# Linear attention with a soft mixture of experts: GpSimd's whole-group operations in halves, x's bias a group ahead, largest logits by way of memory, other ranks

## The chip, the cores and the metric

The kernel runs on one core of a Trainium2 chip. The metric is the device time of one execution in microseconds (us), as the median of several runs. A core has five engines that matter here, each with its own in-order instruction queue: TensorE (PE), VectorE (DVE), ScalarE (ACT), GpSimd (POOL) and SyncE (SP); SP only issues DMA transfers in this kernel. Weight loads of PE are listed apart as PEld.

## The reference

The input x holds 4 sequences of 2048 tokens with 256 channels, all in float32. What is computed, cut to what matters:

```python
def mlp(x, W1, b1, W2, b2): return gelu(x @ W1 + b1) @ W2 + b2          # erf gelu
q, k, v = mlp(x, ..q), mlp(x, ..k), mlp(x, ..v)
scores = einsum('bid,bjd->bij', q, k) / sqrt(256 * 512) * tril(ones)    # no softmax
out = einsum('bij,bjd->bid', scores, v)
out = layernorm(out) * ln_w + ln_b
x = layernorm(x + out)                        # no weights
xn = layernorm(x) * gamma + beta
logits = einsum('bnd,des->bnes', xn/|xn| * scale, mu/|mu|)   # 16 experts x 16 slots
dispatch = softmax(logits, over the tokens n)
combine  = softmax(logits, over all 256 slots)
slot_in  = einsum('bnd,bnes->besd', xn, dispatch)
slot_out = gelu(slot_in @ w1[e] + b1[e]) @ w2[e] + b2[e]     # hidden width 64
out = einsum('besd,bnes->bnd', slot_out, combine)
x = layernorm(x + out)                        # the result, 4 x 2048 x 256
```

The softmax over the tokens needs, for each of the 256 slots, the largest logit of a whole sequence.

## The kernel before

The tokens are worked on in 16 groups of 512 (four groups to a sequence), each group as four tiles of 128 tokens by 256 channels. Attention without a softmax is linear: a running sum of k and v products (`state`) stands for all earlier groups, so that only the 128×128 blocks on the diagonal need scores of their own.

For each group t the kernel calls

- `attend(t)`: the three two-layer networks (first layers L802 on PE, gelu L812 on ACT; second layers L825 for k and L852 for v, taken out of PSUM by DVE at L835 and L863), the scores (L877), the state (L904, L920), the sums of the columns (L937), which go to memory and come back to all partitions (L946, L952, L957, L961) and are added up by GpSimd (L971), and the output (L987, L991), which DVE takes out of PSUM (L1002), measures (L553, L554) and centres and scales with ln_w (L1014);
- `norms(t)`: GpSimd adds ln_b to x in `row` (L1030) and sets a column of ones (L1033); DVE adds the attention to it (L1047); two layer norms follow, of which GpSimd makes the product with gamma (L1106) and the sum with beta (L1114) that give `xn`; ACT takes the sums of the squares (L1125);
- `back(t)`: the logits (L1171) and what the softmaxes need of them (L1193, L1204, L1221), kept negative in `lg`, their smallest values so far in `mx`, and the numerators `ct` of the combine softmax, which are turned round through memory.

After the fourth group of a sequence, `softmaxes(groups)` turns `mx` on PE (L1246), reduces it on DVE to one value for each of the 256 slots (`cm`, two columns of 128 partitions, L1254), and brings these to all partitions: `spread` multiplies the identity by each column (L677, DVE, twice) and multiplies it on PE by a matrix of ones (L683), and ACT copies the product out of PSUM into `dg` (L1271). GpSimd then subtracts `dg` from each group's `lg` (L1282), and ACT takes exp (L1294). `slots` sums over the tokens on PE (L1316), runs the experts (L1368, L1392, L1411, L1438, L1447), and `finish(t)` combines (L1542 on PE, L1550 on DVE), normalises and stores (L1500).

The order of the work isn't written out. Every operation is a step of a planner, `plan.step(engine, length, emit, reads, writes)`, with a rank: `plan.begin(base)` sets the base, and each step takes the base plus 0.01 for each step before it. `Plan.run()` goes through the steps before the program runs, picks for every engine the ready step with the lowest sum of start time and rank times PATIENCE (0 for the engines that compute, where the rank decides between equal starts; 1.0 for SP), with the lengths that the steps carry and an assumed delay LATE from one engine to the next, and so writes down five in-order queues. A step that reads PSUM gets its rank lowered by 1.5. Buffers (`row` has 8 places, `xT` 2, `dg` 1) are given out in the same pass.

The main loop sets the bases; the lines around the change are

```python
attend(t)                                                  # base t
plan.begin(t + (TAIL["norms"] if last else 0.6)); norms(t)
plan.begin(t + 0.3);                              load_x(t + 2)
plan.begin(t + (TAIL["back"] if last else 1.1));  back(t)
```

At the end of a sequence follow `softmaxes` (base t + 1.4), `slots` (t + 1.7) and `finish` of its four groups (from t + 2.6 in steps of 0.2). The last two sequences have bases of their own in TAIL. In the last sequence `softmaxes` is called twice: for its first three groups, and for the last group alone, whose subtraction goes tile by tile to the engines in SUBTRACT. CENTERS says for each of the last eight groups which engine normalises which tile in `finish`. `load_x(t)` issues one load of `row` and eight loads of `xT` on SP.

Of the kernel before, what the change touches and what calls it, by code (L numbers as in the profile page):

```python
# [10 lines left out]
ALU = mybir.AluOpType  # L11
# [6 lines left out]

PIECES = ((2, False), (2, True))

CENTERS = [['ACT', 'ACT', 'ACT', 'ACT'], ['ACT', 'DVE', 'DVE', 'DVE'], ['ACT', 'ACT', 'ACT', 'ACT'], ['DVE', 'DVE', 'DVE', 'DVE'], ['ACT', 'DVE', 'ACT', 'DVE'], ['ACT', 'DVE', 'DVE', 'DVE'], ['ACT', 'ACT', 'ACT', 'ACT'], ['DVE', 'DVE', 'ACT', 'DVE']]

SUBTRACT = ['DVE', 'POOL', 'DVE', 'POOL']

TAIL = {'norms': 0, 'back': 0.3, 'softE': 1.4, 'part': 2.2, 'soft': 1.0, 'slots2': 4.6, 'fin2': [5.5, 0.3], 'slots3': 1.7, 'fin3': [2.6, 0.2], 'table': 1.0}
LAST = 2
W = G * P
LN_EPS = 1e-5
NORM_EPS = 1e-12
# [25 lines left out]

class Plan:

    LATE = {"PE": 0.45, "DVE": 0.25, "ACT": 0.25, "POOL": 0.25, "SP": 3.5, "IN": 0.0}
    TABLE = 1.3

    PATIENCE = {"PE": 0.0, "DVE": 0.0, "ACT": 0.0, "POOL": 0.0, "SP": 1.0, "IN": 0.0}

    def __init__(self):
        self.steps, self.places, self.order, self.free = [], {}, {}, set()
# [16 lines left out]
        self.order[tag].append(b)  # L81
        return b

    def step(self, engine, length, emit, reads=(), writes=(), table=None, holds=()):


        s = Step(engine, length, emit, self.base + self.count, table)
        s.holds = list(holds)
        for b in holds:
            b.left += 1  # L90
        self.count += 0.01

        if any((a[0] if isinstance(a, tuple) else a).tag.startswith("ps_") for a in reads):
            s.rank -= 1.5
        for accesses, write in ((reads, False), (writes, True)):
            for a in accesses:
                b, parts = a if isinstance(a, tuple) else (a, range(a.parts))
                if b not in s.buffers:
                    s.buffers.append(b)
                    b.left += 1  # L100
# [12 lines left out]
        s.before.discard(s)  # L113
        s.waiting = len(s.before)
        for o in s.before:
            o.after.append(s)
        self.steps.append(s)

    def run(self):
# [25 lines left out]
        while left:  # L145
# [43 lines left out]
                    since[b.tag].append(b.last)  # L189
            for o in s.after:  # L190
                o.waiting -= 1
                seen = end + (self.LATE[e] if o.engine != e or e == "SP" else 0.0)
                o.ready = max(o.ready, seen)
                if not o.waiting:
                    ready[o.engine].append(o)
# [8 lines left out]
def _dve(n):  # L204
    return 0.155 + 0.00105 * n


def _pool(n):
    return 0.1 + 0.0022 * n
# [10 lines left out]
def kernel(  # L220
# [43 lines left out]
    for tag, n, shape in (  # L264
# [32 lines left out]
    plan.tag(  # L297
        "bounce", [memory.tile([KC, W, P], F32, name=f"bounce_{i}") for i in range(16)], True
    )
    plan.tag("sums", [memory.tile([G, C], F32, name=f"sums_{i}") for i in range(2)], True)  # L300
    bank_places("mm", 3)
    bank_places("tp", 2)
# [720 lines left out]
    def norms(t):  # L1023
# [1 line left out]


        a, row, mv = a_tiles.pop(t)
        plan.step(
            "POOL", _pool(G * C),
            lambda: nc.gpsimd.tensor_tensor(row[:, :, :C], row[:, :, :C], lnb_r, ALU.add),  # L1030
            [rows_b], [row],
        )
# [11 lines left out]
        for c in range(G):  # L1044

            def emit(c=c):
                nc.vector.scalar_tensor_tensor(  # L1047
                    row[:, c, :C], a[:, c, :], r[:, c : c + 1], row[:, c, :C],
                    ALU.mult, ALU.add, accum_out=mv2[:, c, 0:1] if t >= ACCZ else None,
                )  # L1050

            if t >= ACCZ:
                plan.step("DVE", 0.57, emit, [(a, [c]), r], [(row, [c]), (mv2, [c])])
# [47 lines left out]
                [(row, [c])], [(xn, [c])],  # L1101
            )
        if t < ngroups - 1:
            plan.step(
              "POOL", _pool(G * C),
              lambda: nc.gpsimd.tensor_tensor(  # L1106
                  by_halves(xn), row[:, :, :C].rearrange("p g (k d) -> p k g d", k=KC), gam_h,
                  ALU.mult,
              ),
              [row], [xn],  # L1110
            )
            plan.step(
              "POOL", _pool(G * C),
              lambda: nc.gpsimd.tensor_tensor(by_halves(xn), by_halves(xn), bet_h, ALU.add),  # L1114
              [], [xn],
            )
        plan.step("POOL", 1.4, emit, [rr, ve2], [sq, sc])
        xnT = None
        if by_blocks(t):
# [117 lines left out]
    def softmaxes(groups, before=None):  # L1237
# [22 lines left out]
        if before:  # L1260
# [3 lines left out]
                nc.vector.tensor_tensor(less.place, cm.place, before.place, ALU.subtract)  # L1264

            plan.step("DVE", 0.3, emit, [before], [cm, less])
        row = spread(cm)
        cmb = plan.buffer("dg")
        plan.step(
            "ACT", _act(ES),  # L1270
            lambda: nc.scalar.copy(cmb.place.rearrange("p h e -> p (h e)"), row[:, :ES]),  # L1271
            [row], [cmb],
        )
        for t in groups:

            n = 1 if t == ngroups - 1 else G
            for c in range(0, G, n):
                cs = list(range(c, c + n))
                engine = SUBTRACT[c] if n == 1 else "POOL"

                def emit(lg=l_tiles[t], c=c, n=n, engine=engine):
                    (nc.vector if engine == "DVE" else nc.gpsimd).tensor_tensor(  # L1282
# [4 lines left out]
                        ALU.subtract,  # L1287
                    )

                length = _dve(ES) if engine == "DVE" else _pool(n * ES)  # L1290
                plan.step(engine, length, emit, [cmb], [(l_tiles[t], cs)])

                def emit(lg=l_tiles[t], c=c, n=n):
# [1 line left out]
                        lg[:, c : c + n, :], lg[:, c : c + n, :], AF.Exp, scale=-1.0  # L1295
                    )

                plan.step("ACT", 1.06 if n == G else 0.38, emit, [], [(l_tiles[t], cs)], table="exp")
        if before:
            plan.step(  # L1300
                "ACT", _act(EH),
# [268 lines left out]
    for t in range(ngroups):  # L1570
# [5 lines left out]
        attend(t)  # L1576
        plan.begin(t + (TAIL["norms"] if last else 0.6))
        norms(t)
        plan.begin(t + 0.3)
        load_x(t + 2)  # L1580
        plan.begin(t + (TAIL["back"] if last else 1.1))
        back(t)
        if t == ngroups - 2:

# [5 lines left out]
            kept = part_sums(early)  # L1590
        if t % NG == NG - 1:
            groups = [t] if tail == 2 else list(range(t - NG + 1, t + 1))
            plan.begin(t + (TAIL["soft"] if tail == 2 else 1.4))
            _, less = softmaxes(groups, cm if tail == 2 else None)
            plan.begin(t + (1.7, TAIL["slots2"], TAIL["slots3"])[tail])
            so = slots(groups, kept if tail == 2 else None, less)


            first, by = ((2.6, 0.2), TAIL["fin2"], TAIL["fin3"])[tail]
            for i in range(NG):  # L1600
                plan.begin(t + first + by * i)
                finish(t - NG + 1 + i, so)
# [44 lines left out]
```

## Time and profile before

| | |
|---|---|
| time, median of 3 runs | 663.3 us (662.45 to 664.54) |
| the profiled execution | 663.13 us, span 661.4 us, mean granted PE clock 0.996 |
| busy: PE, DVE, ACT, POOL | 647.2, 490.9, 266.1, 298.5 us |
| L1030, L1106, L1114 (128×1024 on POOL) | 16 of 2.19 us, 15 of 2.18, 15 of 2.37 |
| L1282 (128×1024 on POOL) | 15 of 2.42 us |
| L1014 on DVE (128×256) | 64, mean 0.66 us |
| L683 on PE (ones times `dg`) | 12 records, 3.9 us |
| DMA | 84.7 MB, 128 GB/s over the span |

In a row of the groups of instructions stand the line, the engine, the operation, the tile written and the tile read, the shapes as partitions × elements, and the count; then the busy time in us and the mean of one in ns, and then the time in which the engine stood idle just before them, with what ended it. In a row of the timeline stand the start in us from the beginning of the span, the length in us, the engine, the line, the operation and the count; in brackets the idle time before it and what ended it. In a row of the waits stand who waited for whom, the us in total, how often, and the longest. "SPq" is an issue by SP of a DMA. The chain that ended last is followed back from the last instruction, at each step to what released it. The profile calls an operation on four tiles of a group 128×1024.

### The profile page before, as it was taken

How to read it: one execution, taken by the hardware profiler on the slowest of the kernel's cores; microseconds unless marked ns; L12 is line 12 of the kernel's file. 1: busy time of each engine (PE TensorE's matmuls, PEld its weight loads, DVE VectorE, ACT ScalarE, POOL GpSimd, SP SyncE). 2: the span in 40 equal slices, each digit the busy share in tenths (PEclk: the TensorE clock that was granted, in tenths of full speed). 3: DMA queues.
4: the chain of work that ended last, by engine and by line, in shares of the span. 5: the costliest groups of instructions: out<-in, count | busy, mean ns of one | idle time of the engine just before them, and what ended most of it. 6: DMA issues, size and time to landing. Idle time of an engine off the chain costs nothing.

```text
span 661.4 us, 9366 instructions
## 1 busy us (share of the span) xinstructions
PE 647.2 (98%) x2972; PEld 483.3 (73%) x2972; DVE 490.9 (74%) x1294; ACT 266.1 (40%) x597; POOL 298.5 (45%) x346
## 2 busy tenths in 40 slices
PE   9999999999999999999999999999999999999995
PEld 6657586777768877758686887776767768887874
DVE  1438586979797878778796388996978489886486
ACT  3130515333346227221516323634153544545475
POOL 4343616060739514353426605546061937646234
PEclk9999999999999999999999999999999999999998
DMA  8953655777577095836676525994677372621274
GB/s 247 261 123 109 129 96 130 126 152 158 99 158 128 15 199 174 188 87 128 127 130 136 87 68 91 238 212 104 109 152 133 65 160 70 83 65 32 33 160 160
DMA packets 322233, 84.71 MB, mean 128 GB/s; under 512 B 253068, under 2 KB 319944, under 8 KB 322184
## 3 DMA queue, kind: packets, MB, share of 16 engines
q1 hardware_dynamic: 321080, 83.06, 59.7%
q10 hardware_dynamic: 960, 0.80, 0.4%
q8 instruction: 23, 0.38, 0.2%
q0 software_dynamic: 144, 0.26, 0.1%
q14 instruction: 26, 0.21, 0.1%
HBM read 52.05 MB, written 32.04 MB: 127 GB/s over the span
## 4 chain that ended last, share of the span: by engine, by line
PE 92%; DVE 5%; issue 1%; POOL 1%; POOLq 0%; ACT 0%; DVEq 0%; ACTq 0%
PE mm L802 25%; PE at L904 8%; PE mm L1171 8%; PE mm L852 8%; PE at L1316 8%; PE at L1542 7%; PE at L987 7%; PE mm L825 7%; PE at L877 4%; PE at L991 4%; PE at L937 1%; PE at L461 1%; PE tp L486 1%; DVE xn L1096 1%; PE mm L683 1%
## 5 line engine op out<-in xcount | busy, mean ns | idle before, releaser
L812 ACT ACTIVATE hid<-mm,cols_sb 128x512 f32<-128x512 f32 x96 | 65.1, 686 | 142.1 <-PE mm L802 141.5
L542 POOL TENSOR_TENSOR root<-ve,nhalf 128x4 f32<-128x4 f32 (+1 forms) x39 | 40.7, 1044 | 125.1 <-DVE ve L1037 51.2
L987 PE MATMUL at<-state,hid 128*128 128x256 f32 x240 | 61.6, 379 | 0.0
L904 PE MATMUL at<-vt,kt 128*128 128x256 f32 x240 | 61.3, 385 | 0.0
L825 PE MATMUL mm<-both_sb,hid 128*128 128x257 f32 x256 | 59.5, 381 | 1.4 <-DVE kt L835 1.4
L802 PE MATMUL mm<-xT,W1v_sb 128*128 128x512 f32 x128 | 59.5, 593 | 0.7 <-DVE both_sb L770 0.7
L802 PE MATMUL mm<-xT,W1q_sb 128*128 128x512 f32 x128 | 59.5, 595 | 0.3 <-DVE xT L476 0.3
L1542 PE MATMUL at<-so,ct 128*128 128x256 f32 x256 | 57.9, 381 | 0.8 <-DVE row L1550 0.6
L1316 PE MATMUL at<-row,lg 128*128 128x257 f32 x256 | 58.2, 380 | 0.0
L1171 PE MATMUL mm<-mu_sb,xnT 128*128 128x256 f32 x256 | 58.1, 379 | 0.0
L852 PE MATMUL mm<-W2v_sb,hid 128*128 128x256 f32 x256 | 58.0, 379 | 0.0
L802 PE MATMUL mm<-xT,W1k_sb 128*128 128x512 f32 x128 | 57.7, 593 | 0.0
L825 PEld LDWEIGHTS mm<-both_sb,hid 128*128 128x128 f32 x256 | 48.2, 190 | 9.7 <-DVE kt L835 2.0
L1542 PEld LDWEIGHTS at<-so,ct 128*128 128x128 f32 x256 | 48.0, 190 | 9.9 <-issue 1.7
L1171 PEld LDWEIGHTS mm<-mu_sb,xnT 128*128 128x128 f32 x256 | 48.4, 190 | 8.4 <-issue 1.5
L987 PEld LDWEIGHTS at<-state,hid 128*128 128x128 f32 x240 | 45.6, 190 | 11.8 <-issue 5.7
L1030 POOL TENSOR_TENSOR row<-row,rows_sb 128x1024 f32<-128x1024 f32 x16 | 35.0, 2186 | 42.4 <-DMA row<-in_x_dram 33.9
L852 PEld LDWEIGHTS mm<-W2v_sb,hid 128*128 128x128 f32 x256 | 48.5, 190 | 6.7
L1221 POOL TENSOR_TENSOR sum<-sum,ss 128x4 f32<-128x4 f32 x16 | 4.0, 248 | 109.4 <-DVE ss L1217 92.9
L1316 PEld LDWEIGHTS at<-row,lg 128*128 128x128 f32 x256 | 48.1, 190 | 7.2 <-issue 0.4
L904 PEld LDWEIGHTS at<-vt,kt 128*128 128x128 f32 x240 | 44.4, 190 | 12.0 <-issue 5.4
L946 ACT COPY cs<-at 128x256 f32<-128x256 f32 (+1 forms) x16 | 5.9, 371 | 109.1 <-PE at L937 97.5
(150 smaller groups left out, 1250.8 us busy)
## 6 DMA issues: line engine op xcount, KB each, us to landing
bounce<-xn SPq DMA_DIRECT2D x30, 512.0 KB
row<-in_x_dram SPq DMA_DIRECT2D x16, 512.0 KB
ct<-bounce SPq DMA_DIRECT2D x64, 128.0 KB
bounce<-kt SPq DMA_DIRECT2D x30, 256.0 KB
kT<-bounce SPq DMA_DIRECT2D x60, 128.0 KB
out_dram<-row SPq DMA_DIRECT2D x15, 512.0 KB
xT<-in_x_dram SPq DMA_DIRECT2D x112, 64.0 KB
xnT<-bounce SPq DMA_DIRECT2D x56, 128.0 KB
```

Source lines behind the costliest of these rows:

```text
L542: nc.gpsimd.tensor_tensor(r[:, :n], v[:, :n], nhalf.to_broadcast([P, n]), ALU.pow)
L802: nc.tensor.matmul(ph.place, wa[f"W1{n}"][:, k, m * P : (m + 1) * P], xT[:, k, :], start=(k == 0), stop=(k == KC - 1),)
L812: nc.scalar.activation(hid[n][:, m, :], ph.place, AF.Gelu, bias=cols_sb[:, 4 * i + m : 4 * i + m + 1],)
L825: nc.tensor.matmul(pk[:, : C + 1], hid["k"][:, k, c * P : (c + 1) * P], wqk_sb[:, k, :], start=(k == 0), stop=(k == KC - 1),)
L852: nc.tensor.matmul(pv[:, j * C : (j + 1) * C], hid["v"][:, k, (c0 + j) * P : (c0 + j + 1) * P], wa["W2v"][:, k, :], start=(k == 0), stop=( ...
L877: nc.tensor.matmul(psc[:, toks[c]], kT[:, k, toks[c]], qT[:, k, toks[c]], start=(k == 0), stop=(k == KC - 1),)
L904: nc.tensor.matmul(pds[:, m * C : (m + 1) * C], kt[:, c, m * P : (m + 1) * P], vt[:, c, :], start=True, stop=True,)
L987: nc.tensor.matmul(po[:, :C], qT[:, k, toks[c]], s[:, k, :], start=(k == 0), stop=False,)
L1030: lambda: nc.gpsimd.tensor_tensor(row[:, :, :C], row[:, :, :C], lnb_r, ALU.add),
L1171: nc.tensor.matmul(pl[:, j * ES : (j + 1) * ES], xnT[:, k, (c0 + j) * P : (c0 + j + 1) * P], mu_sb[:, k, :], start=(k == 0), stop=(k == KC ...
L1316: nc.tensor.matmul(psi[:, : C + 1], lg[:, c, h * P : (h + 1) * P], row[:, c, :], start=(i == 0), stop=(i == n - 1),)
L1542: nc.tensor.matmul(pc[:, :C], ct[:, h, c * P : (c + 1) * P], so_t[:, h, :], start=(h == 0), stop=(h == EH - 1),)
```

## The change

Four things are changed.

- GpSimd's operations on a whole group (L1030, L1106, L1114, L1282) become two operations on two tiles each (PART = 2). Multiplication by gamma and addition of beta go half by half. The exp of L1294 is halved with the subtraction. In the last group the third of the four tiles' subtractions moves from DVE to GpSimd.
- The additions of ln_b to x get ranks that are lower by 1.0, a group ahead, and are tracked tile by tile in the planner.
- At the end of the first three sequences the 256 values of `cm` are written to memory by one DMA and read back to all 128 partitions, straight into `dg`, by another, both on SP; `spread` and ACT's copy are left out there. The planner assumes that the write takes 4.5 us longer than an ordinary step of SP. For the last sequence `spread` stays.
- Ranks: steps that read PSUM are lowered by 1.8, not 1.5; DVE's LATE is 0.3, not 0.25; SP's PATIENCE 0.5, not 1.0; `load_x(t + 2)` is at t + 0.8, not 0.3; `back` at t + 1.3, not 1.1; `softmaxes` at 1.6, not 1.4; `slots` at 2.2, not 1.7; `finish` from 2.6 in steps of 0.1, not 0.2. CENTERS has other engines for some tiles.

```diff
-CENTERS = [['ACT', 'ACT', 'ACT', 'ACT'], ['ACT', 'DVE', 'DVE', 'DVE'], ...
-SUBTRACT = ['DVE', 'POOL', 'DVE', 'POOL']
+CENTERS = [['DVE', 'ACT', 'ACT', 'ACT'], ['DVE', 'DVE', 'DVE', 'DVE'], ...
+SUBTRACT = ['DVE', 'POOL', 'POOL', 'POOL']
+PART = 2
...
-    LATE = {"PE": 0.45, "DVE": 0.25, "ACT": 0.25, "POOL": 0.25, "SP": 3.5, "IN": 0.0}
+    LATE = {"PE": 0.45, "DVE": 0.3, "ACT": 0.25, "POOL": 0.25, "SP": 3.5, "IN": 0.0}
-    PATIENCE = {"PE": 0.0, "DVE": 0.0, "ACT": 0.0, "POOL": 0.0, "SP": 1.0, "IN": 0.0}
+    PATIENCE = {"PE": 0.0, "DVE": 0.0, "ACT": 0.0, "POOL": 0.0, "SP": 0.5, "IN": 0.0}
...
-            s.rank -= 1.5
+            s.rank -= 1.8
...
-                seen = end + (self.LATE[e] if o.engine != e or e == "SP" else 0.0)
+                seen = end + s.late + (self.LATE[e] if o.engine != e or e == "SP" else 0.0)
...
+    plan.tag("mins", [memory.tile([EH, P], F32, name=f"mins_{i}") for i in range(2)], True)
...
-        plan.step(
-            "POOL", _pool(G * C),
-            lambda: nc.gpsimd.tensor_tensor(row[:, :, :C], row[:, :, :C], lnb_r, ALU.add),
-            [rows_b], [row],
-        )
+        at = plan.base, plan.count
+        plan.begin(plan.base - 1.0)
+        for c in range(0, G, PART):
+            def emit(c=c):
+                nc.gpsimd.tensor_tensor(
+                    row[:, c : c + PART, :C], row[:, c : c + PART, :C], lnb_r[:, :PART],
+                    ALU.add,
+                )
+            plan.step(
+                "POOL", 1.29, emit, [rows_b], [(row, list(range(c, c + PART)))]
+            )
+        plan.base, plan.count = at
...
+            for c in range(0, G, PART):
+                cs = slice(c, c + PART)
+                def emit_mul(cs=cs):
+                    nc.gpsimd.tensor_tensor(
+                        by_halves(xn)[:, :, cs],
+                        row[:, cs, :C].rearrange("p g (k d) -> p k g d", k=KC),
+                        gam_h[:, :, :PART], ALU.mult,
+                    )
...
+                def emit_add(cs=cs):
+                    nc.gpsimd.tensor_tensor(
+                        by_halves(xn)[:, :, cs], by_halves(xn)[:, :, cs], bet_h[:, :, :PART],
+                        ALU.add,
+                    )
...
-        row = spread(cm)
-        cmb = plan.buffer("dg")
+        if groups[-1] < ngroups - 4:
+            mins, cmb = plan.buffer("mins"), plan.buffer("dg")
+            plan.step(
+                "SP", 0.6,
+                lambda: nc.sync.dma_start(
+                    out=mins.place.rearrange("h p -> p h"), in_=cm.place
+                ),
+                [cm], [mins], late=4.5,
+            )
+            plan.step(
+                "SP", 0.5,
+                lambda: nc.sync.dma_start(
+                    out=cmb.place, in_=mins.place.partition_broadcast(P)
+                ),
+                [mins], [cmb],
+            )
+        else:
+            row = spread(cm)
+            cmb = plan.buffer("dg")
...
-            n = 1 if t == ngroups - 1 else G
+            n = 1 if t == ngroups - 1 else PART
...
-                engine = SUBTRACT[c] if n == 1 else "POOL"
+                engine = SUBTRACT[c] if t == ngroups - 1 else "POOL"
...
-                plan.step("ACT", 1.06 if n == G else 0.38, emit, [], [(l_tiles[t], cs)], table="exp")
+                plan.step("ACT", {1: 0.38, 2: 0.6, 4: 1.06}[n], emit, [], [(l_tiles[t], cs)], table="exp")
...
-        plan.begin(t + 0.3)
+        plan.begin(t + 0.8)
         load_x(t + 2)
-        plan.begin(t + (TAIL["back"] if last else 1.1))
+        plan.begin(t + (TAIL["back"] if last else 1.3))
         back(t)
...
-            plan.begin(t + (TAIL["soft"] if tail == 2 else 1.4))
+            plan.begin(t + (TAIL["soft"] if tail == 2 else 1.6))
...
-            plan.begin(t + (1.7, TAIL["slots2"], TAIL["slots3"])[tail])
+            plan.begin(t + (2.2, TAIL["slots2"], TAIL["slots3"])[tail])
...
-            first, by = ((2.6, 0.2), TAIL["fin2"], TAIL["fin3"])[tail]
+            first, by = ((2.6, 0.1), TAIL["fin2"], TAIL["fin3"])[tail]
```

More of the change, by code (lines that the diff above doesn't have):

```diff
@@ L19 @@
 PIECES = ((2, False), (2, True))
-CENTERS = [['ACT', 'ACT', 'ACT', 'ACT'], ['ACT', 'DVE', 'DVE', 'DVE'], ['ACT', 'ACT', 'ACT', 'ACT'], ['DVE', 'DVE', 'DVE', 'DVE'], ['ACT', 'DVE', 'ACT', 'DVE'], ['ACT', 'DVE', 'DVE', 'DVE'], ['ACT', 'ACT', 'ACT', 'ACT'], ['DVE', 'DVE', 'ACT', 'DVE']]
-SUBTRACT = ['DVE', 'POOL', 'DVE', 'POOL']
+CENTERS = [['DVE', 'ACT', 'ACT', 'ACT'], ['DVE', 'DVE', 'DVE', 'DVE'], ['ACT', 'DVE', 'ACT', 'DVE'], ['ACT', 'DVE', 'ACT', 'DVE'], ['ACT', 'DVE', 'ACT', 'DVE'], ['ACT', 'DVE', 'DVE', 'ACT'], ['DVE', 'ACT', 'ACT', 'ACT'], ['ACT', 'DVE', 'DVE', 'DVE']]
+SUBTRACT = ['DVE', 'POOL', 'POOL', 'POOL']
 TAIL = {'norms': 0, 'back': 0.3, 'softE': 1.4, 'part': 2.2, 'soft': 1.0, 'slots2': 4.6, 'fin2': [5.5, 0.3], 'slots3': 1.7, 'fin3': [2.6, 0.2], 'table': 1.0}
 LAST = 2
+PART = 2
 W = G * P
@@ L82, in buffer, with step @@
         return b
-    def step(self, engine, length, emit, reads=(), writes=(), table=None, holds=()):
+    def step(self, engine, length, emit, reads=(), writes=(), table=None, holds=(), late=0.0):
         s = Step(engine, length, emit, self.base + self.count, table)
-        s.holds = list(holds)
+        s.holds, s.late = list(holds), late
         for b in holds:
@@ L1052, in norms @@
             if t >= ACCZ:
-                plan.step("DVE", 0.57, emit, [(a, [c]), r], [(row, [c]), (mv2, [c])])
+                plan.step(
+                    "DVE", 0.57, emit, [(a, [c]), r], [(row, [c]), (mv2, [c])]
+                )
                 squares_of((row, [c]), mv2, c, lambda c=c: row[:, c, :C])
@@ L1103, in norms @@
         if t < ngroups - 1:
[L1104 to L1116, printed above, removed]
+            for c in range(0, G, PART):
[7 more added lines that the diff above has]
+                plan.step(
+                    "POOL", 1.29, emit_mul, [(row, list(range(c, c + PART)))],
+                    [(xn, list(range(c, c + PART)))],
+                )
[4 more added lines that the diff above has]
+                    )
+                plan.step(
+                    "POOL", 1.29, emit_add, [], [(xn, list(range(c, c + PART)))]
+                )
         plan.step("POOL", 1.4, emit, [rr, ve2], [sq, sc])
@@ L1266, in softmaxes @@
             plan.step("DVE", 0.3, emit, [before], [cm, less])
-        row = spread(cm)
-        cmb = plan.buffer("dg")
[L1269 to L1273, printed above, removed]
+        if groups[-1] < ngroups - 4:
+            mins, cmb = plan.buffer("mins"), plan.buffer("dg")
+            plan.step(
+                "SP", 0.6,
[3 more added lines that the diff above has]
+                [cm], [mins], late=4.5,
+            )
+            plan.step(
+                "SP", 0.5,
[3 more added lines that the diff above has]
+                [mins], [cmb],
+            )
+        else:
+            row = spread(cm)
+            cmb = plan.buffer("dg")
+            plan.step(
+                "ACT", _act(ES),
+                lambda: nc.scalar.copy(cmb.place.rearrange("p h e -> p (h e)"), row[:, :ES]),
+                [row], [cmb],
+            )
         for t in groups:
-            n = 1 if t == ngroups - 1 else G
+            n = 1 if t == ngroups - 1 else PART
             for c in range(0, G, n):
                 cs = list(range(c, c + n))
-                engine = SUBTRACT[c] if n == 1 else "POOL"
+                engine = SUBTRACT[c] if t == ngroups - 1 else "POOL"
                 def emit(lg=l_tiles[t], c=c, n=n, engine=engine):
@@ L1288, in emit @@
                     )
-                length = _dve(ES) if engine == "DVE" else _pool(n * ES)
+                length = _dve(ES) if engine == "DVE" else {1: 0.74, 2: 1.29, 4: 2.24}[n]
                 plan.step(engine, length, emit, [cmb], [(l_tiles[t], cs)])
```

## The prediction

> **What bounds the kernel now.** First the page's busy times, then its chain that ended last:
>
> ```profile
> PE 647.2 (98%) x2972; PEld 483.3 (73%) x2972; DVE 490.9 (74%) x1294; ACT 266.1 (40%) x597; POOL 298.5 (45%) x346
> ...
> PE 92%; DVE 5%; issue 1%; POOL 1%; POOLq 0%; ACT 0%; DVEq 0%; ACTq 0%
> ```
>
> PE works 647.2 of a span of 661.4 us, and the chain is PE's for 92%. The clock is not to gain: 0.996 over the run. Of the 14.2 us in which PE does nothing, about 8 lie behind its last matmul (it ends near 653.2; then the last layer norms and the last store), and those the change doesn't shorten. So the time can fall in two ways only: fewer PE instructions, or fewer PE waits. PE's waits, in us, times, longest:
>
> ```profile
> PE mm L825 <- DVE kt L835: 1.4, 1, 1.4
> PE at L937 <- DVE vt L863: 1.0, 1, 1.0
> PE mm L683 <- DVE dg L677: 0.8, 2, 0.5
> PE mm L802 <- DVE both_sb L770: 0.7, 1, 0.7
> PE at L1542 <- DVE row L1550: 0.6, 1, 0.6
> ```
>
> All are waits for DVE, though DVE is busy 74%. Why is it late? The timeline ahead of the largest one (start, length, engine, line):
>
> ```profile
> 54.62 2.18 POOL L1030 TENSOR_TENSOR row<-row,rows_sb 128x1024 f32<-128x1024 f32 x1 [6.62 <-DMA row<-in_x_dram]
> ...
> 55.26 1.83 DVE L1014 SCALAR_TENSOR_TENSOR a<-a,mv,rows_sb 128x256 f32<-128x256 f32 x1
> ...
> 56.80 2.33 POOL L1030 TENSOR_TENSOR row<-row,rows_sb 128x1024 f32<-128x1024 f32 x1
> 57.01 0.41 DVE L1002 TENSOR_TENSOR a<-at,a 128x256 f32<-128x256 f32 x1
> ...
> 58.13 1.27 DVE L1014 SCALAR_TENSOR_TENSOR a<-a,mv,rows_sb 128x256 f32<-128x256 f32 x1
> ...
> 60.83 0.70 PE L825 MATMUL mm<-both_sb,hid 128*128 128x257 f32 x2 [1.38 <-DVE kt L835]
> ```
>
> The same L1014 takes 0.48 us where GpSimd is idle (61.09). Here two take 1.83 and 1.27 and end just behind the end of a whole-group GpSimd operation: 57.09 behind 56.80, 59.40 behind 59.13. L1002, which reads one operand from PSUM, isn't held. Behind the held pair L835 comes 2.1 us late and PE has nothing. The 1.0 us of L937 at 286.5 has the same cause: L1014 at 278.51 takes 2.33 and one at 284.15 takes 1.70, each inside an L1030. So has the 0.6 at 411.5: L645 at 408.76 takes 1.81 inside L1106 (408.37 to 410.54). From start to start of PE's instructions, the excess over their usual spacing is 1.6 at 60.8, 0.3 at 231.6, 1.25 at 286.5 and 0.9 at 411.5: about 4.1 us, all that can be won from waits in the middle.
>
> **Part 1: halves on GpSimd.** L1030 (16), L1106 (15), L1114 (15) and L1282 (15 of its whole-group form) go in two halves. Price of a half, from these groups (busy, mean ns):
>
> ```profile
> L1030 POOL TENSOR_TENSOR row<-row,rows_sb 128x1024 f32<-128x1024 f32 x16 | 35.0, 2186 | 42.4 <-DMA row<-in_x_dram 33.9 <-PE mm L1171 4.3 <-DMA rows_sb<-in_rows_dram 3.4
> ...
> L971 POOL TENSOR_TENSOR a<-a 128x256 f32<-128x256 f32 x32 | 23.8, 745 | 2.0
> ...
> L696 POOL TENSOR_TENSOR xn<-mu_sb 128x512 f32<-128x512 f32 x1 | 1.0, 1039 | 5.3 <-DMA mu_sb<-in_mu_dram 5.3
> ```
>
> Between 745 ns (256 elements) and 2186 (1024) a straight line gives 1.23 us at 512; the single L696 says 1.04. I take 1.23, which has many rows behind it. The four groups take 139 us today (L1282 35.8, L1114 35.5, L1106 32.7); 122 halves at 1.23 take 150: +11 us on POOL (−12 by L696's price; +17 if L1282 goes by its own line, 0.94 for 256 and 2.42 for 1024, so 1.43). POOL's 298.5 become about 310, under half of the span, so on the path this is nothing, except at the seams priced in part 3. What it brings: a DVE operation caught by GpSimd is held for at most about 1.2 us, not 2.3.
>
> A rule is to be weighed here. The Trainium skill, "SBUF — State Buffer", section "SBUF: two separate sides", says that DVE with two SBUF inputs and GpSimd share one port pair, that whoever starts first has it for the whole instruction, and that the other fully blocks. The rows agree with the block. The rule says nothing on who is next, and if the holder could take it again, halves issued back to back would hold DVE for both, and the 0.9 and 1.0 that I take below for L1014 would be lost: 661.9 in place of 660.0. The row speaks against that: the second L1030 starts at 56.80, and the held L1014 still ends 0.29 us later, not at 59.1. DVE gets its turn between two GpSimd operations. I go by the row; the rule's reading is the first rival.
>
> **Part 2: x's bias a group ahead, and new ranks.** L1030 needs only x's rows and mostly runs as they land (33.9 us of POOL's idle before it end with that DMA), so a higher rank moves it little: in the changed order the last two rows of the first eight are still added beside the L1014 of 55 to 58, now as four halves. There the held time of 1.35 + 0.79 = 2.1 us becomes two or three holds of 0.6 on the mean (half a half), say 1.3: −0.9 of the 1.6. The loads of x half a group later put the other rows elsewhere: −1.0 of 1.25 at 286.5, −0.6 of 0.9 at 411.5 (L1106, halved), −0.2 of 0.3 at 231.6, −0.1 elsewhere. Together −2.8. Bounds: −4.1 (all gone) and 0 (all turn up elsewhere; over the kernel 28 operations are held, some 24 us of DVE, and only these places reach PE); +1 would need more of them before PE though each is shorter.
>
> **Part 3: largest logits by way of memory (three sequences).** Removed for each: two L677 on DVE, two L683 on PE, one L1271 on ACT. On PE, L683 starts at 200.63 and the next L802 at 201.07: 0.44 us, three times −1.3. These lie on PE's path and need no wait to count. DVE gets 3 × 2 × 0.40 = 2.4 us of room, not on the path.
>
> Added: a write of 256 values of 4 B and a read of 128 × 1 KB, both on SP's in-order queue, and the issue order decides when they go. In the timeline at the end of the first sequence:
>
> ```profile
> 198.28 0.38 DVE L1254 TENSOR_REDUCE cm<-tp 128x2 f32<-128x256 f32 x1
> ...
> 201.27 0.37 ACT L1271 COPY dg<-mm 128x256 f32<-128x256 f32 x1 [0.92 <-PE mm L683]
> ...
> 202.53 2.35 POOL L1282 TENSOR_TENSOR lg<-lg,dg 128x1024 f32<-128x1024 f32 x1
> ...
> 209.69 5.60 PE L1316 MATMUL at<-row,lg 128*128 128x257 f32 x25
> ```
>
> In the changed order the write follows the store of xn; then come the four ct loads (2.5 us of issue), the store of the next group's xn, and the eight loads of its xT (203.1 to 208.4 today), and only then the read. So the write lands unseen, at about 201.5, and the read goes at 209.1. Its landing is bounded by two rows: 2.3 us, SP's longest wait for the similar "sums" write, and 4.9, from the issue of a<-sums at 190.19, of the same kind, to L971's start at 195.11. Taken: 2.4, as the xT loads ahead of it are small and nearly through. The Trainium skill, "DMA: Bandwidth & Descriptors", section "Anatomy of one DMA", gives a fixed cost of about 2.0 us to each DMA, and its section "Specifications" has transfers under 512 B done as read-modify-write: two DMAs in a row are then over 4 us against the 3.0 of today's way (198.67 to 201.64). By this the trip is no faster and looks like a loss; it is none as long as the ranks leave room, and they do: L1316 of these sequences moves behind four L825 and two L852 of the next group (3.47 + 3.45 us; in the first also 1.72 of L802). At the first place: T = 211.5, eight halves of 1.25 to 1.3 reach 222 us, and L1316 begins at about 217.9. Its first tiles need one half (1.25), the exp table (1.28), one exp (0.6) and three handovers (0.5), 3.7 us behind T; the later ones come faster (2.5 us a group) than PE uses them (16 × 0.38 = 6.1). So T may be 214.2: margin 2.7. At the second the read follows loads that wait for L802, goes at 366.7, T = 369.4, L1316 at 375.4, latest T 371.7: margin 2.3. By the row of 4.9 the margin is just used up; by the skill's 2.0 it holds with room. The third sequence's L1316 is filler in the tail and waits for nothing. Queued behind the read on SP are the xnT and kT loads; the tightest is kT for L877 (235.2) with about 0.5 us to spare, so 0.3 for the seam of each of the first two sequences, +0.6. Bound: 0 to +1.5 each.
>
> Halving exp (L1294: 1050 ns whole, 418 a quarter, about 0.6 a half) adds 15 × 0.15 = 2.3 us to an ACT busy 40%: hidden; if not, 0.15 each.
>
> **Part 4: head and tail.** In the head two L677 are held today by L1030 (34.74 to 36.95); with halves the first may go sooner and the second be caught: +0.2, from −1 to +1. In the tail SUBTRACT moves one L1282 quarter from DVE (0.69) to POOL (0.94), so the last group's three POOL quarters take 2.8 us in place of 1.9, while L1438 has 7.8 us behind L1411, of which the chain needs about 7.4. CENTERS moves single tiles between ACT and DVE. Net 0, from −0.7 to +1.0.
>
> **Sum.** Against the profiled execution: 663.13 − 1.3 − 2.8 + 0.6 + 0.2 = 659.8. That execution lies 0.2 under the median of the runs (663.3), so 660.0 is the forecast.
>
> **Rivals.** (a) *The holds only move.* Twice as many GpSimd operations, still in front of an in-order DVE; 28 holds today with four that PE feels, another order could have four others. For it: only chance separates held operations that matter from those that don't. Against: each is half as long, and DVE gets its turn between. Time: 663.3 − 1.3 − 0 to 0.6, +0.8 = 662.2 to 662.8. (b) *The read lands too late* (slower). It stands in SP's queue behind eight xT loads, which wait for buffers. Each us past the margin is a us of PE at each of two places. To be slower by 0.3% (2.0 us, about what a measurement of this kernel can tell from no change) against my 660.0 takes 5.3 us, 2.65 at each place beyond a mean margin of 2.5: landing 7.6 us after issue (2.4 + 2.5 + 2.65), half again the 4.9 measured. For it: a load that issues later than planned adds to it (SP waited up to 3.7 us for L802 before xT). Time at that point 665.3, at 10 us after issue about 670. (c) *All stalls go*: −1.3 − 4.1 = 657.9, with no seams. Against: PE at 98% with five in-order queues has always a few tight spots.
>
> **Chances.** Forecast 0.50 (own range 658.6 to 661.3), (c) 0.13, (a) 0.22, (b) 0.15. Faster by over 0.3% (under 661.3): forecast and (c) and a little of (a), 0.64. Slower (over 665.3): (b) nearly whole, 0.14. Same: 0.22. Range: below, (c) with tail at its good end, 657.5; above, all of (a) and the start of (b), 665.0.
>
> **What would show it.** PE busy lower by 1.3 with 6 fewer matmuls; L825's wait at 60 and L937's at 286 gone or under 0.4; no DVE L1014 above 1.4 us; L1030, L1106, L1114 near 1.23 each; POOL near 310 busy; L1316 of the first two sequences with no wait for ACT's exp. It is wrong if PE waits at L1316 for exp, if the halves are near 1.9, if L825, L937 or L1542 wait for DVE elsewhere by over 2 us in sum, or if PE ends at 653 and only the tail is different.

## The result, and the profile after

The changed kernel takes 679.62 us (median of 4 runs, 679.19 to 681.38) against 663.92 of the kernel before: a ratio of 1.0239, with an interval of 1.0219 to 1.026. It is slower by some 16 us, where I had forecast 660.0. The profiled execution has a span of 677.5 us, 16.1 more than before.

Busy times and the chain that ended last, from the page of the changed kernel:

```profile
PE 651.5 (96%) x2966; PEld 483.1 (71%) x2966; DVE 482.8 (71%) x1288; ACT 266.0 (39%) x608; POOL 308.3 (46%) x408
...
PE 75%; DMA 6%; SPq 6%; DVE 5%; POOL 4%; issue 2%; ACT 1%; DVEq 0%; POOLq 0%; ACTq 0%
```

PE issues six matmuls fewer, as it should. But the chain, 92% PE before, is PE's for 75% now; it also runs over DMA (6%), over SP's issues (6%) and over POOL (4%). PE's waits (us, times, longest):

```profile
PE mm L828 <- DVE kt L838: 8.1, 4, 3.0
PE at L994 <- DVE sT L891: 2.4, 1, 2.4
PE mm L1196 <- DVE xnT L537: 2.0, 2, 1.6
PE at L464 <- POOL ident masks.py:199: 1.4, 1, 1.4
PE at L880 <- DVE kT L537: 1.3, 1, 1.3
```

L828 (L825 before) waits for kt four times; three of them, at 214, 376 and 544 us (3.0, 1.7 and 2.8), lie behind the ends of the first three sequences. The timeline shows what stands before the first. SP's issues there:

```profile
198.16 0.37 SPq L1296 DMA_DIRECT2D mins<-cm  x1
198.64 9.93 SPq L530 DMA_DIRECT2D ct<-bounce  x4
209.90 5.05 SPq L341 DMA_DIRECT2D xT<-in_x_dram  x8
215.00 0.49 SPq L1303 DMA_DIRECT2D dg<-mins  x1
```

In the kernel before, the same four loads of ct issue in 2.47 us (at 198.61). Here, behind the write of the largest logits, they take 9.93; at the second and third place 8.52 and 8.72. And here is what DVE and PE make of it, in the same stretch:

```profile
208.39 2.77 PE L828 MATMUL mm<-both_sb,hid 128*128 128x257 f32 x12
211.25 1.25 DVE L537 STREAM_TRANSPOSE ct<-ct 128x1024 f32<-128x1024 f32 x1 [3.98 <-DMA ct<-bounce]
...
213.68 0.76 DVE L838 TENSOR_TENSOR kt<-mm,both_sb 128x257 f32<-128x257 f32 x2
214.16 1.14 PE L828 MATMUL mm<-both_sb,hid 128*128 128x257 f32 x4 [2.99 <-DVE kt L838]
```

DVE stands for 3.98 us at the transpose of ct, with everything else behind it in its queue; L838, which empties PE's bank, is among it. PE then waits for 3.0 us. And that is not all of the price. PE's granted clock, in stretches of 2 us from 212 to 222 (PE, PEld, DVE, ACT and POOL busy, then the clock, the DMA share and GB/s):

```profile
212.00:214.00 2.00, 0.00 (x0) 0.00 (x0) 1.97 (x6) 0.00 (x0) 0.00 (x0) 1.00 0.96 160
214.00:216.00 2.00, 1.84 (x7) 1.62 (x8) 1.97 (x8) 0.00 (x0) 0.00 (x0) 0.86 0.78 123
216.00:218.00 2.00, 2.00 (x6) 1.55 (x5) 1.73 (x4) 0.00 (x0) 0.00 (x0) 0.50 0.73 143
218.00:220.00 2.00, 2.00 (x9) 1.69 (x8) 0.69 (x1) 0.34 (x1) 1.65 (x2) 0.78 1.19 164
```

Behind the wait the clock falls to half, from 215.45 to 218.87 (0.50 over this stretch): 16 of L855 take 5.3 us there, not the 3.45 of L852 in the kernel before.

For the places of a loss I use one more figure, worked out from the trace: the distance from start to start of PE's neighbouring instructions less the usual (median) distance of their kind, summed up. It counts waits and a lower clock alike. In us, by stretches of the program (head to 62 us, middle to 575, tail; the borders are rough where a run is longer):

| kernel | head | middle | tail |
|---|---|---|---|
| before | 6.0 | 18.4 | 5.5 |
| changed | 5.0 | 35.4 | 6.9 |

The loss lies in the middle.

### The profile page after: what moved, and what is told of

Read it like the earlier page. It is cut to its first block, busy times and chain, and to the rows that moved or that the text cites. A ratio compares the mean times of both kernels' runs of the same rounds, so it can differ in the third digit from the quotient of the medians.

```text
span 677.5 us, 9481 instructions
## 1 busy us (share of the span) xinstructions
PE 651.5 (96%) x2966; PEld 483.1 (71%) x2966; DVE 482.8 (71%) x1288; ACT 266.0 (39%) x608; POOL 308.3 (46%) x408
## 4 chain that ended last, share of the span: by engine, by line
PE 75%; DMA 6%; SPq 6%; DVE 5%; POOL 4%; issue 2%; ACT 1%; DVEq 0%; POOLq 0%; ACTq 0%
PE mm L805 17%; PE mm L1196 8%; PE at L1358 8%; PE mm L855 7%; PE at L907 7%; PE mm L828 6%; PE at L1584 6%; PE at L990 6%; SPq L530 5%; PE at L994 3%; PE at L880 3%; DMA bounce<-xn 2%; DMA ct<-bounce 2%; POOL lg L1324 2%; PE at L940 1%
## 5 line engine op out<-in xcount | busy, mean ns | idle before, releaser
L828 PE MATMUL mm<-both_sb,hid 128*128 128x257 f32 x256 | 60.2, 382 | 9.1 <-DVE kt L838 8.1
L828 PEld LDWEIGHTS mm<-both_sb,hid 128*128 128x128 f32 x256 | 48.1, 190 | 19.8 <-DVE kt L838 9.9
L1358 PE MATMUL at<-row,lg 128*128 128x257 f32 x256 | 59.8, 382 | 0.8 <-ACT lg L1336 0.5
L855 PE MATMUL mm<-W2v_sb,hid 128*128 128x256 f32 x256 | 60.0, 387 | 0.0
L1324 POOL TENSOR_TENSOR lg<-lg,dg 128x512 f32<-128x512 f32 (+1 forms) x33 | 40.7, 1269 | 39.8 <-DMA dg<-mins 35.8
L1358 PEld LDWEIGHTS at<-row,lg 128*128 128x128 f32 x256 | 47.7, 190 | 10.0 <-ACT lg L1336 2.9
L855 PEld LDWEIGHTS mm<-W2v_sb,hid 128*128 128x128 f32 x256 | 49.7, 194 | 7.2
L1229 ACT ACTIVATE xn<-lg,nrm 128x256 f32<-128x256 f32 x64 | 31.9, 498 | 56.6 <-DVE lg L1206 56.5
L1036 POOL TENSOR_TENSOR row<-row,rows_sb 128x512 f32<-128x512 f32 x32 | 37.6, 1192 | 15.8 <-DMA row<-in_x_dram 11.2
```

The costliest lines, as they stand in the source:

```text
L828: nc.tensor.matmul(pk[:, : C + 1], hid["k"][:, k, c * P : (c + 1) * P], wqk_sb[:, k, :], start=(k == 0), stop=(k == KC - 1),)
L855: nc.tensor.matmul(pv[:, j * C : (j + 1) * C], hid["v"][:, k, (c0 + j) * P : (c0 + j + 1) * P], wa["W2v"][:, k, :], start=(k == 0), stop=( ...
L1036: nc.gpsimd.tensor_tensor(row[:, c : c + PART, :C], row[:, c : c + PART, :C], lnb_r[:, :PART], ALU.add,)
L1358: nc.tensor.matmul(psi[:, : C + 1], lg[:, c, h * P : (h + 1) * P], row[:, c, :], start=(i == 0), stop=(i == n - 1),)
```

## The experiments

**One part alone, or without one part.** First I took the trip through memory out of the changed kernel, and put each of the three large parts alone into the kernel before. In all four the planner ran anew.

The changed kernel without the trip:

```diff
-        if groups[-1] < ngroups - 4:
+        if False:
```

> The changed kernel with spread (DVE, PE and ACT) at the ends of all sequences, so without the trip through memory; all else as changed. Theory 1, the trip is the loss: the write of 256 values of 4 B holds up the loads of ct behind it, DVE waits for ct, PE for kt; the stalls at 214 (3.2 us and 1.8 of a lower clock), at 376 to 389 (about 5) and at 544 to 550 (about 4.5) go, 1.3 come back for L683: 679.6 - 14.5 + 1.3 = 666.4. Theory 2, the ranks are the loss (loads of x and slots later, SP in another order): the trip is hidden or costs 2 at most, so 677 to 680. Theory 3, the halves on GpSimd are the loss: 677 to 680 too.

Measured: 672.93 us, ratio 1.0145 (1.0125 to 1.0165).

The trip alone, in the kernel before:

```diff
-        row = spread(cm)
-        cmb = plan.buffer("dg")
+        if groups[-1] < ngroups - 4:
+            mins, cmb = plan.buffer("mins"), plan.buffer("dg")
...
```

> The kernel before with the trip through memory alone, for the first three sequences; ranks and whole-group operations as before. Theory 1: each write holds up the loads behind it by about 8 us, and with the old ranks L1316 comes sooner behind the read as well: 663.9 - 1.3 + 3 times 4 to 6 = 675 to 681. Theory 2: the old ranks leave the stalls out, apart from L1316's wait for the read: 663 to 668.

Measured: 688.29 us, ratio 1.038 (1.035 to 1.0409).

The ranks alone, in the kernel before:

```diff
-            s.rank -= 1.5
+            s.rank -= 1.8
...
-        plan.begin(t + 0.3)
+        plan.begin(t + 0.8)
         load_x(t + 2)
...
```

> The kernel before with the new ranks alone (LATE, PATIENCE, PSUM, the bases of load_x, back, softmaxes, slots and finish, CENTERS). Theory 1: only the stalls of the changed kernel that lie away from the three writes can be theirs, at 301 (1.5 us), at 471 (2.6 and 1.8 of clock) and at 578 (1.3): 663.9 + 0 to 7, near 667. Theory 2, the ranks are the loss: 676 to 680. Theory 3: no change, 663 to 665.

Measured: 678.37 us, ratio 1.0224 (1.0196 to 1.0252).

Halves and x's bias alone, planned anew with the old ranks (the changed kernel with spread, and with all ranks, SUBTRACT and CENTERS of before):

```diff
-PATIENCE = {... "SP": 0.5 ...}; s.rank -= 1.8; plan.begin(t + 0.8) ...
+PATIENCE = {... "SP": 1.0 ...}; s.rank -= 1.5; plan.begin(t + 0.3) ...
```

> The kernel before with GpSimd's operations in halves and x's bias a group ahead, no trip through memory and the old ranks. Theories 1 and 2: as predicted, DVE is held for less, PE's waits of 1.4 at 60.8 and of 1.0 at 286.5 shrink: 663.9 - 1 to 3 = 661 to 663. Theory 3, halves are the loss: over 668, with POOL late for somebody.

Measured: 677.32 us, ratio 1.0213 (1.0189 to 1.0237).

No theory had foreseen this: every part alone costs 14 to 25 us, and without the trip the loss is still 9.8. The sum of the three parts (some 54 us) is far from the 16 of the whole, so they don't add up. The places tell why:

| kernel | head | middle | tail |
|---|---|---|---|
| changed, without the trip | 5.2 | 17.0 | 16.1 |
| before, with the trip | 5.8 | 33.4 | 15.2 |
| before, with the ranks | 6.5 | 24.2 | 15.2 |
| before, halves and bias, planned anew | 5.1 | 21.7 | 17.4 |

The middle bears out theory 1: with the trip it is 33 to 35, without it 17 to 24, and the changed kernel without the trip has a middle better than that of the kernel before. But all four lose some 10 to 12 us in the tail, where the changed kernel loses 1.4. The planner makes another tail each time. In the tail of the run with halves and bias:

```profile
640.30 0.38 PE L1453 MATMUL tp<-ident,si 128*128 128x128 f32 x2
640.52 4.48 PE L1584 MATMUL at<-so,ct 128*128 128x256 f32 x20
640.72 0.59 DVE L1461 TENSOR_TENSOR hp<-tp,cols_sb 64x128 f32<-64x128 f32 x2 [0.26 <-PE tp L1453]
...
647.84 1.28 ACT L1472 ACT_TABLE_LOAD   x1
649.14 0.63 ACT L1472 ACTIVATE hz<-hp 64x128 f32<-64x128 f32 x2
...
649.82 1.94 PE L1480 MATMUL at<-w_sb,hz 128*32 128x256 f32 x16 [4.81 <-ACT hz L1472]
```

L1461 has the input of the slot network's gelu ready at 641.3. But the gelu itself, L1472, stands in ACT's queue behind the normalising of other tiles and behind a load of ACT's function table (ACT_TABLE_LOAD), and starts only at 649.14; the 20 matmuls of the combination between the last transposes (L1453) and the second layer (L1480) can't cover that, and PE waits for 4.8 us. In the kernel before, the gelu follows its input at once (L1430 starts at 634.23, L1419 ends at 634.14), and 24 matmuls stand there; in the changed kernel 32. The other three runs have the same place: a table load of 1.28 us just ahead of the last gelu, and a wait of PE for it of 3.8 (without the trip), 4.8 (trip) and 3.6 us (ranks). To see whether it is this order and not the halves, one number of the planner was changed, DVE's assumed delay. In the order that follows, the gelu starts at 633.27, right behind L1461 (633.00) and with no table load, and 28 matmuls stand there:

```diff
-    LATE = {"PE": 0.45, "DVE": 0.25, ...
+    LATE = {"PE": 0.45, "DVE": 0.3, ...
```

> The run with halves and bias, old ranks, and DVE's LATE at 0.3 alone in place of 0.25; in the order that follows, 28 matmuls of L1584 instead of 20 stand between the last transposes of the slots and L1480 (the kernel before has 24). If the 14 us of that run are the tail's order and not the halves: L1480's wait of 4.8 us goes, and with it most of the tail's 12: 665 to 671. If the halves are the loss: 675 to 679.

Measured: 664.65 us, ratio 1.0021 (1.001 to 1.0031); middle 16.8, tail 9.8. The wait at L1480 is gone, and 12.7 us with it and with some in the middle. So the halves weren't the loss; ACT's late gelu in the tail was a large part of it. The lesson on method: where a planner orders everything, taking a part out is another kernel, and says little on the part. From here on the edits leave the order of instructions alone.

**The write, the read, or the place in the queue.** These keep the changed kernel's order. Where zeros are read, or nothing is, the largest logits are left out of the computation. The write as one packet of 1 KB of zeros:

```diff
-                    out=mins.place.rearrange("h p -> p h"), in_=cm.place
+                    out=mins.place.rearrange("h p -> (h p)").unsqueeze(0),
+                    in_=zero[0:1].rearrange("p h e -> p (h e)"),
```

> The changed kernel in its own order of instructions, with one thing other: the write ahead of ct is a single packet of 1 KB of zeros from one partition in place of 256 packets of 4 B, so the logits are shifted by zero (the largest logits are left out of the computation). Theory 1 (the small packets hold up the ct loads): the four ct loads issue in about 2.5 us instead of 8.5 to 9.9, the waits of L828 for kt at 214, 376 and 544 go: 3.2 + 1.8 + 1.9 + 2.9 less, and with what follows up to 3 more: 667 to 670. Rival (it is the place in SP's queue, or a write as such, and not its packets): within 1 of 679.6.

Measured: 665.80 us, ratio 1.0031 (1.0019 to 1.0042); L828's three waits are gone and ct issues in 2.26 us. This write waits for no `cm` and goes out 2.8 us ahead of the ct loads, so by itself the run can't tell the packets from the moment; the runs with 512 B and 64 B below can.

No read, with the write as it is:

```diff
-                lambda: nc.sync.dma_start(
-                    out=cmb.place, in_=mins.place.partition_broadcast(P)
-                ),
+                lambda: None,
```

> The changed kernel with the read of the largest logits left out: GpSimd subtracts a tile of zeros in those three sequences, and the write stays (largest logits left out of the computation). Theory 1: the waits of L828 at 214, 376, 544 stay as they are, only L1358's waits for exp near 382 to 389 go: 677 to 679. Rival of the prediction's own text (the read lands late and that is the loss): 668 or less.

Measured: 677.40 us, ratio 1.0209 (1.0173 to 1.0246). So the late read that I had named as the way to be slower is worth some 2 us at most: its four runs spread from 674.42 to 680.30, and 2 us is not clear of that. The run with one packet puts the write at 14.

The write behind the four ct loads in SP's queue:

```diff
-                lambda: nc.sync.dma_start(
+                lambda: held.append(lambda: nc.sync.dma_start(     # issued after the next ct loads
                     out=mins.place.rearrange("h p -> p h"), in_=cm.place
-                ),
+                )),
```

> The changed kernel with its write of 256 packets of 4 B, which goes behind the four ct loads on SP, not ahead of them. Theory 1 (packets into one 1 KB of memory hold up what is issued behind them for 7 to 8 us): ct is free, and the loads of xT and the read of the largest logits bear it; these have 5 to 8 us of room, so 665 to 672. If the write is harmful wherever it stands, by as much: 677 to 681.

Measured: 674.71 us, ratio 1.0176 (1.0155 to 1.0198), between the two expectations. ct issues in 2.42 us, and the loads of xT behind the write in 10.11, not 5.1. The hold moves to what stands behind the write, and PE then waits for xnT, exp and kt in turn (L1201 1.4 us, L1365 2.0, L833 3.2). The place changes the victim, and only a third of the price.

**What in the write.** The values in pairs, 128 packets of 8 B in place of 256 of 4 B:

```diff
-    memory.tile([EH, P], F32, name=f"mins_{i}")
+    memory.tile([P, EH], F32, name=f"mins_{i}")
...
-                    out=mins.place.rearrange("h p -> p h"), in_=cm.place
+                    out=mins.place, in_=cm.place
```

> The changed kernel with the largest logits laid out in memory as 128 pairs, so that the write has 128 packets of 8 B; GpSimd reads the broadcast tile with a stride of two. The same values are computed. If each small packet costs its turn: the ct loads are held half as long (about 3.5 us instead of 7), most of L828's waits go: 670 to 674. If the delay doesn't depend on the count: as the changed kernel, 678 to 681.

Measured: 663.78 us, ratio 1.0006 (0.9994 to 1.0018), with the same values computed. Next, the 256 values of 4 B at places 512 B apart, beside the one packet:

```diff
+    wide = memory.tile([EH, P, 128], F32, name="wide")
...
+                    nc.sync.dma_start(out=wide[:, :, 0:1].rearrange("h p o -> p h o"), in_=cm.place.unsqueeze(2)),
                     nc.sync.dma_start(out=mins..., in_=zero...),
```

> As the run with one packet, and beside that packet the 256 values of 4 B are written too, each to a place of its own, 512 B apart, which nobody reads. If the small packets are slow because they fall into the same 1 KB of memory one after another: the ct loads go through, and the time is that of the one packet (667 to 670) or 1 to 2 above. If 256 packets of 4 B are slow wherever they go: as the changed kernel, 677 to 682.

Measured: 663.89 us, ratio 1.001 (0.9999 to 1.0021). The same with 64 B between them (`[EH, P, 16]`):

> As the run with the values 512 B apart (one packet of zeros is read, largest logits left out), with the 256 values of 4 B only 64 B apart, so in 16 KB of memory. If the hold comes from packets that fall into the same 64 B: none is left, ct issues in 2.5 us, 663 to 665. If it comes from the same 512 B (8 packets to each): a part or all of the 7.5 us stays, 668 to 680.

Measured: 664.52 us, ratio 1.0015 (1.0001 to 1.0029). And the control, side by side (`[EH, P, 1]`):

> The control to the runs with 512 B and 64 B: the same two writes, with the 256 values side by side in 1 KB that nobody reads. If the place in memory is all that counts: the ct issues take 8 to 10 us again and the time is 677 to 681. If the read of the same 1 KB behind the write has a part in it: below 675.

Measured: 680.81 us, ratio 1.0255 (1.0226 to 1.0284). SP's issues at the first place, in the run with pairs:

```profile
196.72 0.32 SPq L1306 DMA_DIRECT2D mins<-cm  x1
197.14 6.55 SPq L530 DMA_DIRECT2D ct<-bounce  x4
```

in the one with 64 B between the values:

```profile
198.37 0.37 SPq L1300 DMA_DIRECT2D wide<-cm  x1
198.79 0.32 SPq L1304 DMA_DIRECT2D mins<-zero  x1
199.22 2.49 SPq L533 DMA_DIRECT2D ct<-bounce  x4
```

and in the control:

```profile
198.70 0.37 SPq L1300 DMA_DIRECT2D wide<-cm  x1
199.12 0.32 SPq L1304 DMA_DIRECT2D mins<-zero  x1
199.54 8.66 SPq L533 DMA_DIRECT2D ct<-bounce  x4
```

The count of packets (256), their size (4 B) and the bytes are the same in the last two; only the distance in memory differs. Packed into 1 KB they hold what follows, 64 B apart not at all. Over three places the hold (the four ct issues less the 2.3 us that they take in the run with 512 B) is 6.2 to 7.6 us for 256 packets of 4 B, and 2.3 to 4.2 for 128 of 8 B: as an estimate 18 to 33 ns for each. Where does this time go? The DMA engines' GB/s in 40 slices of 0.35 us from 196 to 210, first in the changed kernel, then with 512 B:

```profile
GB/s 288 295 284 151 0 0 0 0 2 1 35 123 159 98 10 0 0 0 1 2 15 20 23 13 26 25 95 57 60 93 25 9 28 34 43 43 27 41 155 192
GB/s 287 297 284 293 163 0 0 0 0 1 5 0 54 165 193 191 176 128 153 173 215 205 176 274 307 313 201 84 152 179 100 110 124 137 165 124 140 142 119 115
```

The 256 small packets themselves are through at once: in the changed kernel's trace they all start between 199.05 and 199.28, and none is recorded as longer than 9 ns. It is the ct packets behind them (128 B each) that then stand still, single ones for up to 2.5 us, where the longest with 64 B takes 0.09. So these runs suggest that many small writes into the same 64 B, or into a smaller unit, wait for one another at a place behind what the packets' records cover, and that the stream behind backs up. How the chip does it stays open, and a distance between 8 and 64 B was not tried.

**What is left of the change.** Without the hold the changed kernel takes what the kernel before takes, though six L683 are gone. In all of these runs L994 waits 3 to 4 us once. In the run with pairs:

```profile
447.61 0.43 SPq L318 DMA_DIRECT2D row<-in_x_dram  x1
448.08 6.15 SPq L530 DMA_DIRECT2D ct<-bounce  x4
...
457.77 1.25 DVE L537 STREAM_TRANSPOSE ct<-ct 128x1024 f32<-128x1024 f32 x1 [7.00 <-DMA ct<-bounce]
...
459.30 0.70 PE L994 MATMUL at<-vt,sT 128*128 128x256 f32 x2 [2.97 <-DVE sT L891]
```

It is the same chain with another cause: in this order a load of x (512 KB) stands directly ahead of ct on SP. One load goes behind:

```diff
         plan.step(
             "SP", {0: 2.5, 1: 6.0, 2: 4.0}.get(t, 0.5),
-            emit, writes=[xt])
+            (lambda: held.append(emit)) if t == ngroups - 1 else emit, writes=[xt],
+        )                                              # held: issued after the next ct loads
```

> The run with pairs of 8 B, and one load moved: the 512 KB of the last group's row go behind the four loads of ct on SP, not ahead of them. If this load is what makes ct late at 448 to 457 (DVE waits 7.0 us for ct, PE 3.0 at L994 for sT): the wait of 3.0 falls under 1, and the time is 660 to 661.5. If the kT loads and the two other rows ahead are the cause: 663 to 664, as the run with pairs.

Measured: 660.36 us, ratio 0.9964 (0.9951 to 0.9976); L1002 (the former L994) waits 0.2 us. The 3.4 us less than with pairs stand on the medians of 12 and 6 executions. The two traces can't show them: the trace with pairs is of the fastest of its 12 (660.77), and there PE's clock stayed at 1.00 behind the wait (458 to 464). With 64 B it fell to 0.50 behind the same wait (462 to 464). Over the executions the mean clock is 0.993 to 0.998 with pairs and 0.997 or 0.998 in all six here, so part of the 3.4 us may be the clock's; that is argued, not shown.

**The halves in the kernel's own order.** Each whole-group operation of the kernel before is issued as two, and nothing is planned anew:

```diff
-            lambda: nc.gpsimd.tensor_tensor(row[:, :, :C], row[:, :, :C], lnb_r, ALU.add),
+            lambda: [nc.gpsimd.tensor_tensor(row[:, c : c + 2, :C], row[:, c : c + 2, :C], lnb_r[:, :2], ALU.add) for c in (0, 2)],
```

> The kernel before in its own order, with each whole-group operation of GpSimd issued as two halves one behind the other; nothing is planned anew. This is the first part of the change alone. As predicted: DVE is caught for half as long, the waits at 60.8 (1.4 us) and 286.5 (1.0) shrink: 663.5 - 1 to 2.5 = 661 to 662.5. Rival (halves back to back hold DVE for as long, or GpSimd's later end matters): 663 to 665. If halves as such are the loss of the run with halves and bias: over 670.

Measured: 661.10 us, ratio 0.9968 (0.9956 to 0.998). DVE's L1014 takes at most 1.49 us, where it took 2.35. PE's waits of this run (its L1031 is the former L1030):

```profile
PE mm L683 <- DVE dg L677: 1.5, 3, 0.8
PE at L461 <- POOL ident masks.py:199: 1.4, 1, 1.4
PE mm L825 <- DVE kt L835: 1.2, 1, 1.2
```

The waits at 286.5 and 411.5 are gone. The one at 60.55 stays, at 1.2:

```profile
55.09 2.49 POOL L1031 TENSOR_TENSOR row<-row,rows_sb 128x512 f32<-128x512 f32 x2 [4.87 <-DMA row<-in_x_dram]
55.15 1.49 DVE L1014 SCALAR_TENSOR_TENSOR a<-a,mv,rows_sb 128x256 f32<-128x256 f32 x1
...
57.59 2.49 POOL L1031 TENSOR_TENSOR row<-row,rows_sb 128x512 f32<-128x512 f32 x2
57.69 1.45 DVE L1014 SCALAR_TENSOR_TENSOR a<-a,mv,rows_sb 128x256 f32<-128x256 f32 x1
```

Each L1014 starts just behind a first half and waits for nearly all of it; it ends at 56.64 and 59.14, and the second halves at 57.58 and 60.08. This answers the question that the prediction weighed: DVE gets its turn between two halves issued back to back.

## Why the prediction was wrong

**The step that failed** is in part 3, "So the write lands unseen, at about 201.5". I had priced the write by its own landing and by who waits for it (nobody), and not by what it does to the transfers behind it. It held the ct loads for 6.2 to 7.6 us at each of three places; through DVE's in-order queue this reached PE. Its price, with the order kept: 679.62 against 663.89 and 664.52 with the same packets apart, 15 us, nearly the whole loss. Of the rule of small transfers (the Trainium skill, "DMA: Bandwidth & Descriptors", section "Specifications") I took only the latency and weighed that against the margin of L1316; the runs with 64 B and 512 B show that smallness alone holds up nothing here. It takes many of them in one place. Whether the read-modify-write of that rule is what makes them wait isn't shown.

**The read** was sized at 2.4 us from issue to POOL's start; it is 3.35 in the changed kernel (215.00 to 218.35) and 3.5 with the one packet. The section "Anatomy of one DMA" of that page gives its fixed 2.0 us for DMAs that GpSimd issues; this one is SP's, and the measured 3.35 decides. With the write mended the margin held: PE doesn't wait at L1358 in the runs with one packet, pairs or 512 B.

**The rival on the slower side (b)** had the sign right, and its mechanism wrong: the late read is worth some 2 us at most, by the run without it.

**L683**: six matmuls fewer, as said.

**Halves**: forecast 1.23 us, measured:

```profile
L1134 POOL TENSOR_TENSOR xn<-xn,rows_sb 128x512 f32<-128x512 f32 x30 | 38.4, 1280 | 2.4
L1324 POOL TENSOR_TENSOR lg<-lg,dg 128x512 f32<-128x512 f32 x30 | 38.4, 1315 | 35.8 <-DMA dg<-mins 35.8
L1036 POOL TENSOR_TENSOR row<-row,rows_sb 128x512 f32<-128x512 f32 x32 | 37.6, 1192 | 15.8 <-DMA row<-in_x_dram 11.2 <-DMA rows_sb<-in_rows_dram 4.0 <-PE tp L489 0.6
```

POOL is busy for 308.3 us; about 310 was forecast. In their own order the halves bring 2.2 us (663.26 to 661.10), where −2.8 was taken for halves and ranks together. The place was partly wrong: I took 0.9 at 60.8, and it brought 0.2; the waits at 286.5 and 411.5 went wholly. That no L1014 would be above 1.4 us was set too low (1.49 here, 1.57 in the changed kernel): a hold of about 1.1 on top of its own 0.48.

**Ranks**: I took them as a way to spread the holds, with 0 as the worst end. In the changed kernel's order a load of x stands directly ahead of ct, worth 3.4 us (663.78 to 660.36), a term that the sum had not. The ranks alone don't put it there: with the same ranks and no trip these ct loads issue at 437.54, ahead of kT, in 2.17 us. Planned into the kernel before they cost 15, with ACT's late gelu in it. The seams of +0.6 for the xnT and kT loads can't be told apart in the runs.

**Head and tail** came to 1.4 more in the tail and 1.0 less in the head: the head at the good end of its bounds, the tail 0.4 outside (+1.0). The 7.8 us that I gave L1438 behind L1411 don't stand in the timeline of the kernel before, where they start at 638.43 and 632.93, 5.5 us apart.

With the two faults on SP's queue taken away, the kernel takes 660.36; the sum of the other steps had said 660.0. That they are so close is luck in part. In its trace (661.39 us, against 663.13 before) the excess is 5.4, 19.4 and 4.9, 29.7 us in sum, against 29.9 before: beyond the six matmuls (1.3) hardly anything of the 2.8 is seen. PE waits at 58.6 (1.1 us), behind two L1025 (the former L1014) of 1.40 and 1.23, at 308.7 (1.2), behind one of 1.42, and at 470.3 (1.1). So holds did move to other places, as rival (a) said, and how much of the 2.8 came in this order stays open.

## What to carry to other kernels

A tiny DMA is priced by what stands behind it on its queue. When a column over the partitions is written to memory, many 4 B packets into one small stretch hold up what is issued behind them. Spread them, or pair them, which halved the hold here or nearly so (what turning the column into a row would cost wasn't measured), and look whether the next transfers' issues get longer. In a kernel that a planner orders, test one part with the order held fixed: one constant of the planner moved 12.7 us here, more than all parts that were meant to help.

## What the runs showed of the hardware

- 256 writes of 4 B into 1 KB held the loads behind them for 6.2 to 7.6 us; the same 256 writes 64 B or 512 B apart did not (ct issues in 2.5 and 2.3 us).
- A PE that stood for 3.0 us got a clock of 0.50 for 3.4 us afterwards (215.45 to 218.87), which cost 1.85 us more. It came again behind the 2.4 us at 470.88, but not behind the 2.8 us at 544.75, nor behind 3.5 us at 473.68 in the control, so the length of the wait alone doesn't decide.
- GpSimd's 128×512 add takes 1.19 us and a 128×1024 one 2.19: two halves cost about 0.2 us more than one whole.
- A DVE operation that a GpSimd half held was done 0.3 us behind that half (56.64 and 56.35), with the next half already running: it got its turn between the two.
